# Attention over normalized tokens: merging the query and key projections, moving the value projection behind the softmax, and moving one routing step

## The chip, the cores and the metric

The kernel runs on one core of one Trainium2 chip. The metric is the device time of one execution in microseconds, the median over runs. A core has four compute engines, each with its own instruction queue that is worked off in order: TensorE (PE in the profile; PEld are its weight loads), VectorE (DVE), ScalarE (ACT) and GpSimd (POOL). SyncE (SP) here only issues DMAs. Queues wait for each other through semaphores. Matmuls write to PSUM; everything else lives in SBUF.

## What is computed

The input x is 2 x 64 x 64 tokens of 128 channels in float32. Four layers follow one another, each adding to x: a local attention with relative positions (layer 0), a triangular multiplication (layer 1), a gated causal attention and a feed-forward part in which 64 experts choose tokens (layer 2), and the layer of this study, layer 3. Its two halves, with t the tokens as 2 x 4096 x 128:

```python
def _L3_attn_ref(x, Wq, bq, Wk, bk, Wv, bv):
    TEMP = (2 * 128) ** 0.5
    q = jnp.einsum('bnf,of->bno', x, Wq) + bq
    k = jnp.einsum('bnf,of->bno', x, Wk) + bk
    v = jnp.einsum('bnf,of->bno', x, Wv) + bv
    scores = jnp.einsum('bnf,bmf->bnm', q, k) / TEMP
    alpha = jax.nn.softmax(scores, axis=-1)
    return jnp.einsum('bnm,bmf->bnf', alpha, v)

def _L3_ffn_ref(x, router_w, router_b, expert_w, expert_b):
    router_probs = jax.nn.softmax(x @ router_w + router_b, axis=-1)
    top_p, top_i = jax.lax.top_k(router_probs, K)          # K = 2 of E = 8
    top_p = top_p / jnp.sum(top_p, axis=-1, keepdims=True)
    expert_out = jnp.einsum('bnd,edc->bnec', x, expert_w) + expert_b
    gathered = jnp.take_along_axis(expert_out, top_i[..., None], axis=2)
    return jnp.einsum('bnk,bnkc->bnc', top_p, gathered)

t = t + _L3_attn_ref(_ln_t(t), ...)     # _ln_t: (v - mean) / sqrt(var + 1e-5)
t = t + _L3_ffn_ref(_ln_t(t), ...)
```

The attention has one head of width 128, is not causal, and has no output projection.

## The kernel before

**x stays in SBUF** for the whole kernel as `self.x`, 64 chunks of 128 tokens (128 partitions) by 128 channels. Constants: P = C = 128, L = 4096 tokens a batch, B = 2 batches, NC = 32 chunks and NB = 8 blocks of 512 tokens a batch, E2 = 8 experts. All matmuls are float32; the trace shows each of them as two passes, so that a matmul counts as x2.

**Layer 3's weights** are made early. `layers` (L1700 to L1734) opens a small pool at the start of layer 1, loads Wq, Wk, Wv and the biases on SP's queue ahead of layer 1's own weights, transposes the three matrices on TensorE after layer 1 was recorded (L1728 to L1731), and calls `l3_bound` (L1769 to L1810). This computes from the weights a bound on any score, so that the softmax may leave out the maximum. A register gets the answer; `layer3` (L1736 on) branches on it at L1763 between `l3_bounded`, which runs here, and `l3_any`, a general path that takes a softmax by rows.

**Layer 2's attention** (`layer2_attn`) is written with generators: its key groups, positions, block ends and so on are jobs, added by `add(key, pieces, generator)` in the loop at L1480 and following, and a planner lets a piece run between score steps according to how much is left (the pieces are costs, the loop's end is the due time). The order of the instructions on each engine is fixed by that when the program is built.

**Layer 3's attention** (`l3_bounded`, L1942 to L2076) walks over 2 batches x 8 blocks of 512 queries. Within a block there are 16 steps `k2`, each with two chunks of keys:
- scores: two matmuls at L2048 from kT (128 channels x 128 keys) and qT (512 queries) into the PSUM tile `sc`;
- exponentials on ACT at L2059 into `es` (three buffers, the first step's being the accumulator `acc`);
- of the step before (`values`, L2001 on): two matmuls at L2008 that add v^T es to the PSUM tile `oT`, and a DVE addition at L2016 that sums `es` into `acc` for the denominators.

Then `piece()` lets one step of the first waiting job run (two in the first block). The jobs:
- `keys` (`l3_qkv`, L1834): for a group of 512 tokens, statistics on DVE with a square root on ACT (`l3_stats`), normalization on DVE and four transposes on TensorE (`l3_transposed`, L1831) with a copy by ACT, then two projections (L1846, tiles `pk` and `pq`) with a bias pass by ACT each, and four matmuls for the values (L1853, tile `pv`) with an addition of bv by DVE at L1856. Batch 0's eight groups run in the first block, batch 1's one by one in the blocks of batch 0.
- `end` (L1974): DVE copies `oT`, GpSimd adds the two halves of `acc` (L1979, tile `both`), TensorE transposes the outputs back to tokens (L1983, tile `po`) and sums the denominators over partitions (L1986, `pr`), and DVE scales and adds to x (L1997).
- `logits` (`f3_logits`, L1860): statistics, normalization and transposes of the finished block, kept in `self.xnT`, and the router matmul (L1876).
- `route` (`f3_route`): the choice of two experts of 8 by maxima on DVE and an exponential on ACT; for 32 chunks of batch 0, for 28 of batch 1.
- `bias` (`f3_bias`, L1926): the chosen weights are copied by GpSimd into a padded tile, transposed (L1933), copied by ACT (L1935) and multiplied with the experts' biases (L1938); DVE adds the result to x (L1940).

After the last block the waiting jobs are run to their end, and then (L2071 to L2076) come `f3_route` for the last four chunks and the `f3_bias` of the last block.

**The experts** (`l3_experts`, L2127 on) take the 64 chunks one after the other. For each, two matmuls at L2142 make all eight experts' outputs in one two-bank PSUM tile `ex` (four buffers); DVE adds experts 0 to 3 with their weights to x (L2151, four instructions); ACT scales experts 4 to 7 into `y` (L2156, four); GpSimd sums these and adds them to x (L2162 to L2164); every fourth chunk 256 KB are written out.

Of the kernel before, what the change touches and what calls it, by code (L numbers as in the profile page):

```python
# [15 lines left out]
B = 2  # L16
# [23 lines left out]
class Net:  # L40
# [1022 lines left out]
    def layer2(self, kept, done):  # L1063
        nc, tc, ins = self.nc, self.tc, self.ins
        with tc.tile_pool(reuse_waits="tile", name="g2", bufs=1) as gp:
# [13 lines left out]
            self.layer2_attn(gate, kept)  # L1079
# [3 lines left out]
    def layer2_attn(self, gate, kept):  # L1083
# [4 lines left out]
        with ExitStack() as st:  # L1088
# [400 lines left out]
            for i, (b, qb) in enumerate(order):  # L1489
                finish(("prepare", i))  # L1490
                nk = 4 * qb + 4
                if i == 0:
                    for g in range(1, NB):
                        add(("keys", 0, g), 3, keys(0, g, add_back=(g == 7)))
                    add(("sums", 0), 0, add_up(0))
                if i == 4:
                    add(("stats", 1), 0, norm_stats(1))
# [202 lines left out]
    def layers(self):  # L1700
# [9 lines left out]
        with tc.tile_pool(reuse_waits="tile", name="l3w", bufs=1, side="right") as wp:  # L1710
            w = {}
            kp = kept.enter_context(
                tc.tile_pool(reuse_waits="tile", name="l12", bufs=1, side="right")
            )
            with (
                tc.tile_pool(reuse_waits="tile", name="l3s", bufs=1) as ap,
                tc.tile_pool(reuse_waits="tile", name="l3sp", bufs=1, space=PSUM) as ps,
            ):
                raw = {n: self.load(ap, f"r{n}", [P, C], ins[f"L3_attn_W{n}"]) for n in "qkv"}
                for n in "qk":  # L1720
                    w[f"b{n}"] = self.load(wp, f"b{n}", [P, 1], column(ins[f"L3_attn_b{n}"]))
                w["bv"] = self.load(wp, "bv", [P, C], row_bcast(ins["L3_attn_bv"], C))
                w["rw"] = self.load(wp, "rw", [P, E2], ins["L3_ffn_router_w"])
                w["rb"] = self.load(wp, "rb", [P, E2], row_bcast(ins["L3_ffn_router_b"], E2))
                space = self.layer1(xT, gst, na, nb, xp, kp)
                for n in "qkv":
                    pt = ps.tile([P, C], F32, tag="misc", name=f"l3w{n}")
                    nc.tensor.transpose(pt, raw[n], self.ident)  # L1728
                    w[n] = wp.tile([P, C], F32, tag=f"w{n}", name=f"l3w{n}T")
                    nc.scalar.copy(w[n], pt)  # L1730
                small = self.l3_bound(ap, ps, raw, w)  # L1731
            first.close()
            self.layer2(space, kept.close)
            self.layer3(w, small)  # L1734

    def layer3(self, weights, small):  # L1736
        nc, tc, ins = self.nc, self.tc, self.ins
        G = B * NC
        with ExitStack() as st:
# [23 lines left out]
            with tc.If(small > 0) as fits:  # L1763
                self.l3_bounded(weights)
# [4 lines left out]
    def l3_bound(self, ap, ps, raw, weights):  # L1769
# [6 lines left out]
        nc = self.nc  # L1776
        ab = ap.tile([P, 2, C], F32, tag="ab", name="l3ab")
        for i, (lhsT, rhs) in enumerate(((raw["k"], raw["q"]), (None, None))):
            m = ps.tile([P, C], F32, tag="misc", name=f"l3m{i}")
            if i:  # L1780
                lhsT = rhs = ab[:, 0, :]
            nc.tensor.matmul(m, lhsT=lhsT, rhs=rhs, start=True, stop=True)
            nc.vector.tensor_copy(ab[:, i, :], m)
        pv = ps.tile([P, 4], F32, tag="misc", name="l3mv")
        bq, bk = weights["bq"], weights["bk"]
        nc.tensor.matmul(pv[:, 0:1], lhsT=raw["q"], rhs=bk, start=True, stop=True)
        nc.tensor.matmul(pv[:, 1:2], lhsT=raw["k"], rhs=bq, start=True, stop=True)
        bb = ap.tile([P, 4], F32, tag="bb", name="l3bb")
        nc.vector.tensor_copy(bb[:, 0:2], pv[:, 0:2])
        nc.vector.tensor_tensor(bb[:, 0:2], bb[:, 0:2], bb[:, 0:2], ALU.mult)  # L1790
        nc.vector.tensor_tensor(bb[:, 2:3], bq, bk, ALU.mult)
        nc.vector.tensor_tensor(ab[:, 0, :], ab[:, 1, :], ab[:, 1, :], ALU.mult)
        nc.vector.tensor_reduce(bb[:, 3:4], ab[:, 0, :], AX.X, ALU.add)
        ones = ap.tile([P, 1], F32, tag="one", name="l3one")
        nc.vector.memset(ones, 1.0)
        pt = ps.tile([P, 4], F32, tag="misc", name="l3mt")
        nc.tensor.matmul(pt[:1], lhsT=ones, rhs=bb, start=True, stop=True)
        t = self.small.tile([1, 4], F32, tag="l3t", name="l3t", bufs=1)
        nc.vector.tensor_copy(t, pt[:1])
        total = self.small.tile([1, 1], F32, tag="bs1", name="l3s1")  # L1800
        root = self.small.tile([1, 1], F32, tag="bs2", name="l3s2")
        nc.vector.tensor_tensor(total, t[:, 2:3], t[:, 2:3], ALU.mult)
        nc.vector.tensor_tensor(t[:, 0:1], t[:, 0:1], t[:, 1:2], ALU.add)
        nc.vector.tensor_scalar(t[:, 0:1], t[:, 0:1], float(C), None, ALU.mult)
        nc.vector.tensor_tensor(total, total, t[:, 0:1], ALU.add)
        nc.vector.tensor_scalar(total, total, 15.0, None, ALU.mult)
        nc.scalar.activation(root, t[:, 3:4], AF.Sqrt)
        nc.vector.tensor_scalar(root, root, 1.25 * C * C, None, ALU.mult)
        nc.vector.tensor_tensor(total, total, root, ALU.add)
        return self.at_most("l3", total, 60.0**2 * 2.0 * C)  # L1810
# [13 lines left out]
    def l3_transposed(self, ap, ps, out, n0, mv, r, tag):  # L1824
# [3 lines left out]
        xn = ap.tile([P, 4, C], F32, tag="xn", name=f"{tag}xn", bufs=2)  # L1828
# [5 lines left out]
    def l3_qkv(self, ap, ps, w, b, g, qT, kT, v, tag):  # L1834
# [3 lines left out]
        n0 = b * NC + 4 * g  # L1838
        mv, r = self.l3_stats(ap, n0, t)
        yield  # L1840
        xT = ap.tile([P, 512], F32, tag="xT", name=f"{t}xT", bufs=2)
        self.l3_transposed(ap, ps, xT, n0, mv, r, t)
        yield
        for dst, n in ((kT, "k"), (qT, "q")):
            pq = ps.tile([P, 512], F32, tag="misc", name=f"{t}p{n}")
            nc.tensor.matmul(pq, lhsT=w[n], rhs=xT, start=True, stop=True)  # L1846
            nc.scalar.activation(
                dst[:, g * 512 : (g + 1) * 512], pq, AF.Identity, bias=w[f"b{n}"]
            )
            yield  # L1850
        pv = ps.tile([P, 4, C], F32, tag="misc", name=f"{t}pv")
        for i in range(4):
            nc.tensor.matmul(  # L1853
                pv[:, i, :], lhsT=xT[:, i * P : (i + 1) * P], rhs=w["v"], start=True, stop=True
            )
        nc.vector.tensor_tensor(  # L1856
            v[:, 4 * g : 4 * g + 4, :],
            pv,
            w["bv"].unsqueeze(1).broadcast_to([P, 4, C]),
            ALU.add,  # L1860
        )
# [81 lines left out]
    def l3_bounded(self, w):  # L1943
# [7 lines left out]
        with (  # L1951
# [22 lines left out]
            def end(b, qb, oT, acc):  # L1974
# [7 lines left out]
                for i in range(4):  # L1982
                    nc.tensor.transpose(po[:, i, :], os[:, i * P : (i + 1) * P], self.ident)  # L1983
# [20 lines left out]
            def values():  # L2004
# [12 lines left out]
                if k2 == NC // 2 - 1:  # L2017
# [6 lines left out]
                    jobs["logits", b, qb] = self.f3_logits(ap, ps, w, b, qb, "f3f")  # L2024
# [46 lines left out]
            for job in (  # L2071
                self.f3_route(ap, 2 * NC - 4, 4, "f3r2"),
                self.f3_bias(ap, ps, w, 2 * NB - 1, "f3f"),
# [137 lines left out]
```

## Time and profile before

| what | value |
|---|---|
| median of 3 runs | 4906.94 us (4905.28 to 4908.01) |
| the profiled execution | 4914.85 us |
| its span in the trace | 4913.0 us |
| mean granted TensorE clock | 0.954 |
| layer 0 | 0 to about 2173 us |
| layer 1 | to about 2368 us |
| layer 2, attention / feed-forward | to about 3620 / 3780 us |
| layer 3, attention | to about 4767 us |
| layer 3, rest of routing and biases | to about 4789.8 us |
| layer 3, experts and output | to the end |

The profile is of one execution. Its page gives, by engine, the busy time, then groups of instructions: line, engine, operation, output and inputs, shape and count, then after the first bar the busy time and the mean duration in ns, and after the second the idle time of the engine just before these instructions with what ended it. Where the idle time is 0.0 the engine went from one instruction to the next. The rows by stage give a window in us, its length, the busy time of PE, PEld, DVE, ACT and POOL with their counts, the granted clock as a share of full speed, the DMA share and GB/s. The chain of waits gives a start, a length and what ran or was waited for; "issue" is time for which the profile shows no wait.

### The profile page before, as it was taken

To read this page: it belongs to the slowest core of one execution; us is meant where nothing else is said; L and a number is where in the kernel's file an instruction comes from. 1 tells how busy PE (TensorE), PEld (TensorE's weight loads), DVE (VectorE), ACT (ScalarE), POOL (GpSimd) and SP (SyncE) were. 2 spreads that over 40 slices of the span, in tenths; PEclk is the share of its full clock that TensorE was granted. 3 is DMA by queue.
4 is the path that set the end of the run, shared out by engine and by line. 5 is a ranking of instruction groups with operands and counts; after the bars stand their busy time and mean duration, and the time that the engine had idled before them with its cause. 6 is when DMAs were issued, how large, how long until landed. Compare 5 with 4: busy or idle time off the path is not lost.

```text
span 4913.0 us, 78463 instructions
## 1 busy us (share of the span) xinstructions
PE 4556.6 (93%) x33360; PEld 1785.9 (36%) x33360; DVE 2937.1 (60%) x4864; ACT 2666.8 (54%) x3100; POOL 922.1 (19%) x832
## 2 busy tenths in 40 slices
PE   6999999999999999977789999999967999999999
PEld 4333333333233333325322223222225444444443
DVE  4676767676766767774755666555553444454447
ACT  4555555555656555555567766676631443333335
POOL 1000000000000000003355555555520000000008
PEclk7999999999999999988899999999978999999999
DMA  1000000000000000000000000000034000000001
GB/s 46 10 1 10 1 10 1 10 1 10 1 1 10 1 12 1 1 8 16 8 1 1 1 1 1 1 1 1 1 106 176 0 1 1 0 1 0 0 1 35
DMA packets 43355, 60.30 MB, mean 12 GB/s; under 512 B 4496, under 2 KB 25200, under 8 KB 41840
## 3 DMA queue, kind: packets, MB, share of 16 engines
q1 hardware_dynamic: 41696, 54.34, 3.5%
q8 instruction: 265, 4.34, 0.4%
q10 hardware_dynamic: 1296, 0.82, 0.1%
q14 instruction: 98, 0.80, 0.1%
HBM read 42.57 MB, written 4.19 MB: 10 GB/s over the span
## 4 chain that ended last, share of the span: by engine, by line
PE 38%; DVE 6%; ACT 3%; POOL 3%; issue 2%; DMA 0%; POOLq 0%; DVEq 0%; ACTq 0%
PE scl L2048 9%; PE oTl L2008 9%; PE l2sc L1422 5%; PE l2pos L1180 4%; PE l2av L1468 3%; PE f3ex L2142 2%; DVE l2es L1442 2%; POOL l2es L1445 2%; ACT l2es L1453 1%; ACT l2es L1433 1%; PE l2po L1388 1%; DVE l2a L169 0%; PE f3fpb L1938 0%; PE l2pu L1180 0%; PE f2pp L1613 0%
## 5 line engine op out<-in xcount | busy, mean ns | idle before, releaser
L597 DVE TENSOR_TENSOR l0es<-l0es,l0ew 128x1024 f32<-128x1024 f32 x1024 | 1251.9, 1227 | 603.3 <-ACT l0es L596 603.3
L596 ACT ACTIVATE l0es<-l0sc 128x1024 f32<-128x1024 f32 x1024 | 1043.5, 1024 | 721.9 <-PE l0sc L588 712.3
L546 PE MATMUL l0o<-l0es,l0v 64*33 64x512 f32 x8192 | 1069.8, 592 | 51.7 <-DVE l0os L556 46.4
L588 PE MATMUL l0sc<-l0qa,ka 64*64 64x512 f32 x8192 | 1081.9, 597 | 4.7 <-ACT l0es L596 4.6
L1453 ACT ACTIVATE l2es<-l2es 128x1024 f32<-128x1024 f32 (+3 forms) x576 | 560.0, 984 | 274.7 <-POOL l2es L1445 266.8
L1445 POOL TENSOR_TENSOR l2es<-l2es 128x1024 f32<-128x1024 f32 (+3 forms) x352 | 581.4, 1662 | 489.4 <-DVE l2es L1442 417.3
L2016 DVE TENSOR_TENSOR accl<-accl,esl 128x1024 f32<-128x1024 f32 x240 | 293.8, 1224 | 430.4 <-ACT esl L2059 426.5
L1442 DVE TENSOR_SCALAR l2es<-l2sc 128x1024 f32<-128x1024 f32 (+3 forms) x320 | 338.6, 1058 | 316.4 <-PE l2sc L1422 313.6
L2059 ACT ACTIVATE esl<-scl 128x1024 f32<-128x1024 f32 x240 | 245.8, 1024 | 472.5 <-PE scl L2048 446.7
L546 PEld LDWEIGHTS l0o<-l0es,l0v 64*33 64x33 f32 x8192 | 257.9, 108 | 659.4 <-issue 564.3
L588 PEld LDWEIGHTS l0sc<-l0qa,ka 64*64 64x64 f32 x8192 | 294.8, 133 | 547.4 <-issue 480.9
L2048 PE MATMUL scl<-l3qT,l3kT 128*128 128x512 f32 x1024 | 486.3, 595 | 0.0
L1422 PE MATMUL l2sc<-l2q,kept 32*128 32x512 f32 (+3 forms) x2304 | 391.7, 628 | 83.3 <-ACT l2es L1433 63.3
L2008 PE MATMUL oTl<-esl,l3v 128*128 128x512 f32 x960 | 450.9, 592 | 0.0
L722 POOL TENSOR_TENSOR x<-x,l0y 128x256 f32<-128x256 f32 x32 | 23.4, 732 | 2074.4 <-DVE l0y L717 1945.9
L1468 PE MATMUL l2av<-l2es,kept 128*32 128x512 f32 (+3 forms) x2304 | 314.8, 594 | 0.0
L1180 PE MATMUL l2pos<-kept 128*32 128x512 f32 x2416 | 297.3, 600 | 0.0
L2008 PEld LDWEIGHTS oTl<-esl,l3v 128*128 128x128 f32 x960 | 181.8, 190 | 225.8 <-issue 222.9
L2048 PEld LDWEIGHTS scl<-l3qT,l3kT 128*128 128x128 f32 x1024 | 186.9, 190 | 199.8 <-issue 186.0
L1433 ACT ACTIVATE l2es<-l2sc 128x1024 f32<-128x1024 f32 x224 | 226.4, 1010 | 48.6 <-PE l2sc L1422 47.1
L1422 PEld LDWEIGHTS l2sc<-l2q,kept 32*128 32x128 f32 x2304 | 117.1, 189 | 327.3 <-ACT l2es L1433 165.3
L1979 POOL TENSOR_TENSOR bothl<-accl 128x512 f32<-128x512 f32 x16 | 20.2, 1265 | 799.2 <-DVE accl L2016 799.2
(733 smaller groups left out, 3882.0 us busy)
## 6 DMA issues: line engine op xcount, KB each, us to landing
f2w<-in_L_ffn_weight_dram SPq DMA_DIRECT2D x32, 1024.0 KB, 13.5
l0ew<-l0ew SPq DMA_DIRECT2D x16, 512.0 KB, 5.1
x<-in_x_dram SPq DMA_DIRECT2D x8, 512.0 KB, 8.9
out_dram<-x SPq DMA_DIRECT2D x16, 256.0 KB, 2.3
kept<-in_L_attn_pos_rev_dram SPq DMA_DIRECT2D x1, 1792.0 KB
ew<-in_L_ffn_expert_w_dram SPq DMA_DIRECT2D x1, 512.0 KB, 4.0
kept<-in_L_attn_pos_rev_dram SPq DMA_DIRECT2D x1, 256.0 KB, 3.1
f2b<-in_L_ffn_weight_dram ACTq DMA_DIRECT2D x2, 128.0 KB, 2.5
```

What stands on the lines that cost most here:

```text
L546: nc.tensor.matmul(o[64 * h : 64 * h + HD + 1, r, :], lhsT=v1[rows, k, 2 * pair + h, :], rhs=es[rows, h, :], start=(k == 0), stop=(k == NC ...
L588: nc.tensor.matmul(sc[64 * c : 64 * c + 64, h, :], lhsT=ka[rows, k0 : k0 + 64], rhs=qa[rows, k // (NC // 2), qs], start=True, stop=True,)
L596: nc.scalar.activation(es, sc, AF.Exp)
L597: nc.vector.tensor_tensor(es, es, ew[:, :, qs], ALU.mult)
L1180: nc.tensor.matmul(out[part], lhsT=lhsT[:, part], rhs=rhs, start=start, stop=stop)
L1422: nc.tensor.matmul(sc[:, h2, off:], lhsT=kT[hs, k * P : (k + 1) * P], rhs=q[hs, off:], start=True, stop=True,)
L1442: nc.vector.tensor_scalar(es[:, :, lo:], sc[:, :, lo:], root, None, ALU.mult)
L1445: nc.gpsimd.tensor_tensor(part, part, part, ALU.mult)
L1453: nc.scalar.activation(es[:, :, off:], es[:, :, off:], AF.Silu)
L1468: nc.tensor.matmul(avs[i][hs, off:], lhsT=v[:, k, hs], rhs=es[h // 2][:, h % 2, off:], start=(k == 0), stop=last,)
L2008: nc.tensor.matmul(oT, lhsT=vs[b][:, k, :], rhs=es[:, i, :], start=(k == 0), stop=(k == NC - 1),)
L2048: nc.tensor.matmul(sc[:, i, :], lhsT=kTs[b][:, k * P : (k + 1) * P], rhs=qT[:, qb * 512 : (qb + 1) * 512], start=True, stop=True,)
```

## The change

With xn the normalized tokens, the scores are (Wq xn_i + bq) . (Wk xn_j + bk). Terms without j fall out of the softmax over j, which leaves (Wk^T Wq xn_i + Wk^T bq) . xn_j. So the keys can be xn itself, and one projection of the queries by the product of the two matrices holds all. In the same way Wv can be applied to the weighted sum of xn instead of to each xn, and bv, which is weighted by shares that sum to one, is added to x once.

The change does this in five places.
- `layers` no longer loads Wq, Wk, Wv, bq and bk at the start of layer 1 and no longer transposes or bounds there; `l3_bound` is gone. A new job `l3_weights` of four pieces in layer 2's attention, added at its third block (i == 2), loads them into space of layer 2's kept tile and makes Wv^T, Wq^T Wk and Wk^T bq, and a new bound from the latter two, without a square root. The register is loaded in its last pieces.
- `l3_qkv`: the normalized tokens are written straight into `v`, their transposes are copied into `kT`, one projection makes `qT`. GpSimd adds bv to x, 128 x 512.
- `end`: the four transposes of `po` become four matmuls with Wv^T on the right.
- The last block's `logits`, `route` and `bias` leave `l3_bounded`. A new generator `f3_late` holds them, and `l3_experts` runs one step of it ahead of every odd chunk.
- In `l3_experts` the PSUM tile `ex` has three buffers instead of four; two banks serve the late job.

`l3_any` is adapted as well; it doesn't run here.

```diff
+    def l3_weights(self, ap, ps, w, take):
+        nc, ins = self.nc, self.ins
+        raw = {n: take([C]) for n in "qkv"}
+        for n in "qkv":
+            nc.sync.dma_start(out=raw[n], in_=ins[f"L3_attn_W{n}"])
+        bq = self.load(ap, "rbq", [P, 1], column(ins["L3_attn_bq"]))
+        yield
+        pt = ps.tile([P, 512], F32, tag="misc", name="l3wps")
+        nc.tensor.transpose(pt[:, :C], raw["v"], self.ident)
+        nc.tensor.matmul(pt[:, C : 2 * C], lhsT=raw["q"], rhs=raw["k"], start=True, stop=True)
+        nc.tensor.matmul(pt[:, 2 * C : 2 * C + 1], lhsT=raw["k"], rhs=bq, start=True, stop=True)
+        nc.vector.tensor_copy(w["v"], pt[:, :C])
+        nc.vector.tensor_copy(w["qk"], pt[:, C : 2 * C])
+        nc.vector.tensor_copy(w["bqk"], pt[:, 2 * C : 2 * C + 1])
+        yield
+        pt = ps.tile([P, 512], F32, tag="misc", name="l3nps")
+        nc.tensor.matmul(pt[:, :C], lhsT=w["qk"], rhs=w["qk"], start=True, stop=True)
...
+        ok = self.small.tile([1, 1], mybir.dt.int32, tag="bok", name="bok_l3")
+        nc.vector.tensor_scalar(ok, t[:, 0:1], 0.0, None, ALU.is_gt)
+        yield
+        yield
+        w["small"] = nc.values_load(
...
     def l3_qkv(self, ap, ps, w, b, g, qT, kT, v, tag):
...
+        cols = slice(g * 512, (g + 1) * 512)
         mv, r = self.l3_stats(ap, n0, t)
         yield
-        xT = ap.tile([P, 512], F32, tag="xT", name=f"{t}xT", bufs=2)
-        self.l3_transposed(ap, ps, xT, n0, mv, r, t)
+        self.l3_transposed(ap, ps, kT[:, cols], n0, mv, r, t, v[:, 4 * g : 4 * g + 4, :])
         yield
-        for dst, n in ((kT, "k"), (qT, "q")):
-            pq = ps.tile([P, 512], F32, tag="misc", name=f"{t}p{n}")
-            nc.tensor.matmul(pq, lhsT=w[n], rhs=xT, start=True, stop=True)
...
-        pv = ps.tile([P, 4, C], F32, tag="misc", name=f"{t}pv")
...
+        pq = ps.tile([P, 512], F32, tag="misc", name=f"{t}pq")
+        nc.tensor.matmul(pq, lhsT=w["qk"], rhs=kT[:, cols], start=True, stop=True)
+        nc.scalar.activation(qT[:, cols], pq, AF.Identity, bias=w["bqk"])
+        xs = self.x[:, n0 : n0 + 4, :]
+        nc.gpsimd.tensor_tensor(xs, xs, w["bv"].unsqueeze(1).broadcast_to([P, 4, C]), ALU.add)
         yield
...
                 for i in range(4):
-                    nc.tensor.transpose(po[:, i, :], os[:, i * P : (i + 1) * P], self.ident)
+                    nc.tensor.matmul(
+                        po[:, i, :],
+                        lhsT=os[:, i * P : (i + 1) * P],
+                        rhs=w["v"],
+                        start=True,
+                        stop=True,
+                    )
...
-                    jobs["logits", b, qb] = self.f3_logits(ap, ps, w, b, qb, "f3f")
+                    if (b, qb) != (B - 1, NB - 1):
+                        jobs["logits", b, qb] = self.f3_logits(ap, ps, w, b, qb, "f3f")
...
             while jobs:
                 piece()
-            for job in (
-                self.f3_route(ap, 2 * NC - 4, 4, "f3r2"),
-                self.f3_bias(ap, ps, w, 2 * NB - 1, "f3f"),
-            ):
-                for _ in job:
-                    pass
...
+    def f3_late(self, ap, ps, w):
+
+        g4 = B * NC // 4 - 1
+        yield from self.f3_logits(ap, ps, w, B - 1, NC // 4 - 1, "f3l")
+        yield from self.f3_route(ap, 4 * g4, 4, "f3l")
+        yield from self.f3_bias(ap, ps, w, g4, "f3l")
...
-            tc.tile_pool(reuse_waits="tile", name="f3p", bufs=4, space=PSUM) as ps,
+            tc.tile_pool(reuse_waits="tile", name="f3p", bufs=2, space=PSUM) as ps,
+            tc.tile_pool(reuse_waits="tile", name="f3b", bufs=1) as bp,
         ):
+            late = self.f3_late(bp, ps, w)
             for n in range(B * NC):
+                if n % 2:
+                    next(late, None)
                 b, k = divmod(n, NC)
-                ex = ps.tile([P, E2, C], F32, tag="ex", name=f"f3ex{n}")
+                ex = ps.tile([P, E2, C], F32, tag="ex", name=f"f3ex{n}", bufs=3)
```

## The prediction

> **What bounds the kernel now.** I read the page's engine totals and costliest groups first, then busy time by stage, then the chain of waits in one stretch of layer 3's attention and at its end.
>
> ```profile
> PE 4556.6 (93%) x33360; PEld 1785.9 (36%) x33360; DVE 2937.1 (60%) x4864; ACT 2666.8 (54%) x3100; POOL 922.1 (19%) x832
> ...
> L2016 DVE TENSOR_TENSOR accl<-accl,esl 128x1024 f32<-128x1024 f32 x240 | 293.8, 1224 | 430.4 <-ACT esl L2059 426.5
> ...
> L2048 PE MATMUL scl<-l3qT,l3kT 128*128 128x512 f32 x1024 | 486.3, 595 | 0.0
> L1422 PE MATMUL l2sc<-l2q,kept 32*128 32x512 f32 (+3 forms) x2304 | 391.7, 628 | 83.3 <-ACT l2es L1433 63.3
> L2008 PE MATMUL oTl<-esl,l3v 128*128 128x512 f32 x960 | 450.9, 592 | 0.0
> ...
> L1979 POOL TENSOR_TENSOR bothl<-accl 128x512 f32<-128x512 f32 x16 | 20.2, 1265 | 799.2 <-DVE accl L2016 799.2
> ```
>
> Both big matmul groups of layer 3 (L2048, L2008) have no idle time before them; layer 2's scores (L1422) do wait. The stages, with PE, PEld, DVE, ACT and POOL busy and then the granted clock:
>
> ```profile
> 2640.00:2960.00 320.00, 295.94 (x2271) 92.81 (x2260) 191.85 (x399) 223.44 (x237) 174.05 (x113) 0.96 0.00 1
> ...
> 3872.00:4357.00 485.00, 485.00 (x1344) 230.88 (x1344) 227.89 (x576) 195.36 (x209) 11.76 (x10) 1.00 0.00 1
> 4357.00:4762.00 405.00, 405.00 (x1074) 189.09 (x1074) 178.09 (x379) 138.56 (x147) 11.45 (x14) 1.00 0.00 0
> 4762.00:4790.00 28.00, 18.65 (x59) 8.29 (x58) 13.89 (x53) 6.63 (x14) 2.53 (x7) 0.90 0.01 2
> 4790.00:4913.00 123.00, 112.34 (x256) 49.22 (x256) 89.81 (x256) 73.22 (x256) 102.23 (x192) 0.96 0.12 35
> ```
>
> Layer 3's attention is TensorE alone, every microsecond of it, at full clock, with DVE under half busy and ACT at 40%. A microsecond of PE taken out there is one off the kernel. The chain while the first block makes its keys (start, us, what):
>
> ```profile
> 3822.77 1.72 PE oTl L2008 x4
> 3824.49 0.44 PE l3f_4t L1831 x4
> 3824.93 1.72 PE scl L2048 x4
> 3826.65 1.72 PE oTl L2008 x4
> 3828.36 0.86 PE l3f_4pk L1846 x2
> 3829.22 0.86 PE l3f_4pq L1846 x2
> 3830.08 1.08 PE l3f_4pv L1853 x8
> 3831.16 1.72 PE scl L2048 x4
> ```
>
> A group of 512 keys costs 0.44 + 0.86 + 0.86 + 1.08 = 3.24 us beside its four 1.72 us pieces. The end of the attention:
>
> ```profile
> 4779.85 0.45 PE f3f_7t L1831 x4
> ...
> 4788.06 0.70 DVE x L1940
> 4788.76 1.00 issue
> 4789.76 10.45 PE f3ex L2142 x18
> ```
>
> From the last block's transposes to the first expert matmul, one serial chain (logits, choice, bias) runs with nothing beside it.
>
> **The change part by part.** The profiled execution took 4914.85 us, its span 4913.0. The median of the runs is 4906.94, so I make the sum on the profiled one and take it off the median.
>
> Attention, keys. Each of 16 groups loses one projection (0.86) and the value projection (1.08): 16 x 1.94 = -31.0. One ACT pass (0.69) and one DVE add (0.69) go too, beside PE work, for nothing. At the block ends, four transposes (0.44) become matmuls by Wv in the form of the value projection (1.08): 16 x 0.64 = +10.3. **Sum -20.8.** It checks on a block: a block of batch 0 is 16 x 3.434 (scores and values) + 3.24 (keys) + 0.79 + 0.44 (end) + 1.23 (logits) = 60.6, and L1979 starts every 60.65. After, 59.3; in batch 1 57.4 becomes 58.0; the first block sheds 15.5. In that block a score now waits on transposes, ACT's copy (0.59), one projection and one ACT pass (0.69); the transposes stand a score pair ahead of their use, so the copies hide behind 1.72 us pieces. Were they exposed in each of the 8 groups, it would be 8 x 0.6 = +5 at most.
>
> GpSimd's adds. The value bias goes into x on GpSimd, 128x512, 16 times; the nearest row is L1979 at 1.265. GpSimd is nearly idle there (11.8 of 485), and x is needed only at its block's end. Here a rule speaks against the change: the Trainium skill, "SBUF — State Buffer", section "Who interferes with whom", says that a DVE instruction with two SBUF inputs and a GpSimd instruction that reads SBUF exclude each other, one waiting for the whole of the other. The accumulation L2016 has two SBUF inputs. L1979 never runs beside it (it waits for it), so no row shows this. By L1979's row the 16 adds cost nothing; by the rule, if each delay reached PE, 16 x 1.265 = +20, the whole gain. I take 0: DVE is 47% busy, an accumulation has 3.4 us and takes 1.22, and three buffers stand between it and ACT. Bounds 0 to +20, by the slack near 0.
>
> Tail. Before, the last bias of the waiting seven ends in a DVE add at 4780.58, then come logits, choice and bias until 4788.75, then 1.00 us to the first expert matmul. After, the seven biases follow the block end directly: +0.64 for Wv (counted above), then the same 1.6 us apiece, so the add ends at 4780.6 on the old clock and experts start near 4781.7. **-8.1.**
>
> Experts. The last block's statistics, logits, choice and bias now run there: PE +2.2 (0.44 + 0.79 + 0.12 + 0.86), DVE +6.4 by their rows in the tail, POOL +0.2, and ACT a square-root and an exp table load (1.28 each). Their PSUM buffers fall from 4 to 3. In steady state a tile takes PE 1.72, DVE 4 x 0.351 plus issue = 1.51, POOL 0.73 + 0.46 + 0.46 with issue = 1.75, without gaps from the second tile: GpSimd is the bound, PE 0.03 behind. A buffer lives 3.2 us past its matmuls (DVE 0.2 + 1.51, ACT 0.1 + 1.14, release 0.25) against 2 x 1.72 = 3.43 with three: 0.23 slack, where four had 1.95. So what DVE does late goes through to GpSimd. At the start, DVE does the statistics (3.75 with the wait for ACT) before its first tile, and I get GpSimd's first add 6.7 us after the first matmul, where it was 6.6. In tiles 4 to 7 logits and choice put 2 to 2.5 us on DVE, in tiles 12 to 15 the bias 0.9 on PE and 0.7 on DVE. Against that stands the start: the first twelve expert matmuls took 0.85 apiece instead of 0.43 (4.9 us), of which GpSimd saw about 1.1 as a gap. The skill's "TensorE: Matmul & The Clock Gate", "What's actually happening", has the clock halve after an idle window of about 3.4 us. Before, PE stood still 3.0, 0.4 and 1.7 us between 4782 and 4790; after, once, about 1.7. By the rows (a gap halves it) the start stays slow and costs nothing new; by the rule it keeps its clock and GpSimd wins the 1.1. I take the 1.1: +3.3 - 1.1 = **+2**, between -2 and +8.
>
> Layer 1's start. Its seven loads, the transposes, the bound and their DVE and ACT steps leave. DVE sets the time there until 2208; about 1.1 us of l3ab and l3bb copies and of a wait for the square root stand in its queue: **-1.1** (0 to -2). The weight loads stand in another order on SP's queue (two of the five wide ones now behind bv, rw, rb, some 1.3 us later, just ahead of their use).
>
> Layer 2. The weights' product is made there: 0.9 us of PE, 2.6 of DVE, three loads on SP ahead of layer 2's own (issued around 2342, behind a 23.6 us pair; layer 2's first waits for other work until 2366.4, which hides them; uncovered, 3 x 0.45 = 1.4). PE's queue is in order, so a small matmul that waits for a DVE copy holds the scores behind it, 0 to 1.5 us twice. More than that, the job moves the planner's other pieces through the layer. PE is 92% busy there; its waits are 83 us. A shift is as likely to save as to cost; bounds -4 to +6, taken **+1**.
>
> Sum: -20.8 - 8.1 + 2 - 1.1 + 1 = **-27**. On the profiled execution 4888; from the median 4906.9 - 27 = **4880**.
>
> **The rivals.** The experts give the tail back: with 0.23 us of slack every late piece of DVE passes through, and +8 comes in place of +2: 4886. For it: the buffer's arithmetic. Against: late pieces lie apart, one step every second tile.
>
> The port: accumulations wait on GpSimd's adds and ACT and PE with them: -27 + 20 = 4900. Against: half of DVE is idle.
>
> Slower: layer 2's schedule falls out of step. Its L1422 waits of 83.3 us grow by half, +41.6, since pieces come between squared scores and their release (L1433): 4921. From +27 it eats the gain. Against: four small pieces among thousands of matmuls.
>
> It does not take the bounded path: the new test compares (1.25 C^2)^2 times the squared norm of the Gram matrix with the bias side squared. Worked from the inputs these are 1.7e11 and 8.5e11, so it passes. Failing would be far slower (a softmax by 128 queries with transposed probabilities); under 1 in 100.
>
> **How the numbers follow.** 0.2% of this kernel, 10 us, is about what a measurement can tell from no change. Forecast, 4872 to 4887: 63%. Layer 2 or a warm expert start gain more, down to 4867: 12%. The experts give back more or part of the keys' gain is exposed, 4887 to 4897: 17%. The port or a worse schedule, 4897 to 4917: 5%. Slower: 3%. Faster 0.92, same 0.05, slower 0.03. The range 4867 to 4893 leaves out some 15 in 100.
>
> **What would show it.** In the first block the key groups lie 8.16 us apart (10.10 before), blocks 59.3 and 58.0, L2048 and L2008 still with no idle time; the accumulation still at 1.22. The first expert matmul comes about 8 us sooner after the last block, GpSimd shows gaps near tiles 4 to 7, and the stage from there is 2 us longer. I am wrong if PE idles in the first block, if the accumulation stretches beside GpSimd, or if layer 2 moves by over 6 us.

## The result and the profile after

The changed kernel takes 4879.43 us, the median of 4 runs (4875.38 to 4883.02), against 4907.48 (4905.28 to 4911.56) for the kernel before, measured again beside it: a ratio of 0.994, 95% interval 0.9928 to 0.9952. That is 28.1 us less; the forecast was 4880, 27 less.

Its profiled execution took 4879.15 us with a span of 4877.3. The page's lines that answer to those of before:

```profile
PE 4514.3 (93%) x33260; PEld 1766.5 (36%) x33260; DVE 2943.3 (60%) x4845; ACT 2647.6 (54%) x3077; POOL 943.7 (19%) x848
...
L2014 DVE TENSOR_TENSOR accl<-accl,esl 128x1024 f32<-128x1024 f32 x240 | 302.6, 1261 | 425.8 <-ACT esl L2058 422.4
...
L2047 PE MATMUL scl<-l3qT,l3kT 128*128 128x512 f32 x1024 | 486.8, 595 | 0.0
L1422 PE MATMUL l2sc<-l2q,kept 32*128 32x512 f32 (+3 forms) x2304 | 389.4, 619 | 88.6 <-ACT l2es L1433 65.3
L2006 PE MATMUL oTl<-esl,l3v 128*128 128x512 f32 x960 | 450.9, 592 | 0.0
...
L1971 POOL TENSOR_TENSOR bothl<-accl 128x512 f32<-128x512 f32 x16 | 20.2, 1263 | 633.6 <-DVE accl L2014 633.6
```

TensorE has still no idle time in layer 3's attention (the 0.0 of L2047 and L2006), so it has only less to do. The accumulation's mean rose from 1224 to 1261 ns: something stands in its way that wasn't there before. Layer 2's scores wait 88.6 us instead of 83.3. The stages (window, length, then busy time of PE, PEld, DVE, ACT, POOL, then the granted clock):

```profile
2398.00:3606.00 1208.00, 1102.57 (x8171) 352.66 (x8167) 717.38 (x1327) 838.18 (x891) 660.50 (x462) 0.95 0.00 1
...
3783.00:4732.50 949.50, 949.50 (x2570) 448.15 (x2571) 444.98 (x1051) 361.17 (x389) 44.44 (x39) 1.00 0.00 0
4732.50:4752.70 20.20, 14.69 (x47) 6.35 (x46) 8.04 (x14) 4.09 (x9) 2.31 (x6) 1.00 0.01 3
4752.70:4877.30 124.60, 114.51 (x271) 50.46 (x271) 94.99 (x296) 75.17 (x262) 102.35 (x193) 0.96 0.12 35
```

To compare stages between kernels I use marks that all have: the ends of layer 0's and layer 2's scores, the first and last score of layer 3, and the first expert matmul. One execution each:

| stage | before | after | difference |
|---|---|---|---|
| layer 0's last value matmul to layer 1's main projection | 74.8 | 69.2 | -5.6 |
| from there to layer 2's first score | 163.0 | 161.9 | -1.1 |
| layer 2, first to last score | 1207.3 | 1207.5 | +0.2 |
| to layer 3's first score | 179.6 | 177.6 | -2.0 |
| layer 3, first to last score | 970.5 | 949.6 | -20.9 |
| to the first expert matmul | 27.6 | 20.2 | -7.4 |
| experts, to the end of the span | 123.2 | 124.6 | +1.4 |

Layer 0's end differs by 0.3. The lines from layer 2's scores on sum to -28.7, close to the timed difference of -28.1. Layer 1's -5.6 and the -1.1 behind it come on top in these two executions; the profiled one of before was 7.4 us above its median, that of the changed kernel at its median. An experiment below goes into that.

In the first block the chain of waits of the changed kernel reads:

```profile
3801.58 0.44 PE l3f_3t L1836 x4
3802.01 1.72 PE scl L2047 x4
3803.73 1.72 PE oTl L2006 x4
3805.45 0.86 PE l3f_3pq L1850 x2
3806.31 1.72 PE scl L2047 x4
3808.02 1.72 PE oTl L2006 x4
3809.74 0.44 PE l3f_4t L1836 x4
```

A key group comes every 8.16 us, as forecast, and TensorE goes from one piece to the next without a gap. The end of the attention:

```profile
4749.20 1.14 PE f3fpb L1930 x2
4750.34 0.02 issue
4750.36 0.70 DVE x L1932
4751.06 1.66 issue
4752.72 7.08 PE f3ex L2156 x12
4759.81 0.44 PE f3l_7t L1836 x4
```

The experts follow the seventh bias, with no choice in between, but 1.66 us after its addition (`issue`: the profile shows nothing that is waited for). The last block's transposes now stand between expert matmuls.

### The profile page after: what moved, and what is told of

Read it like the earlier page. It is cut to its first block, busy times and chain, and to the rows that moved or that the text cites. A ratio compares the mean times of both kernels' runs of the same rounds, so it can differ in the third digit from the quotient of the medians.

```text
span 4877.3 us, 78242 instructions
## 1 busy us (share of the span) xinstructions
PE 4514.3 (93%) x33260; PEld 1766.5 (36%) x33260; DVE 2943.3 (60%) x4845; ACT 2647.6 (54%) x3077; POOL 943.7 (19%) x848
## 4 chain that ended last, share of the span: by engine, by line
PE 37%; DVE 6%; ACT 3%; POOL 3%; issue 2%; DMA 0%; POOLq 0%; DVEq 0%; ACTq 0%
PE scl L2047 9%; PE oTl L2006 9%; PE l2sc L1422 5%; PE l2pos L1180 4%; PE l2av L1468 3%; PE f3ex L2156 2%; DVE l2es L1442 2%; POOL l2es L1445 2%; ACT l2es L1453 1%; ACT l2es L1433 1%; PE l2po L1388 1%; DVE l2a L169 0%; PE f3fpb L1930 0%; PE pol L1975 0%; PE l2pu L1180 0%
## 5 line engine op out<-in xcount | busy, mean ns | idle before, releaser
L2014 DVE TENSOR_TENSOR accl<-accl,esl 128x1024 f32<-128x1024 f32 x240 | 302.6, 1261 | 425.8 <-ACT esl L2058 422.4
L2047 PE MATMUL scl<-l3qT,l3kT 128*128 128x512 f32 x1024 | 486.8, 595 | 0.0
L1422 PE MATMUL l2sc<-l2q,kept 32*128 32x512 f32 (+3 forms) x2304 | 389.4, 619 | 88.6 <-ACT l2es L1433 65.3
L2006 PE MATMUL oTl<-esl,l3v 128*128 128x512 f32 x960 | 450.9, 592 | 0.0
L2047 PEld LDWEIGHTS scl<-l3qT,l3kT 128*128 128x128 f32 x1024 | 188.5, 191 | 208.2 <-issue 192.5
L2006 PEld LDWEIGHTS oTl<-esl,l3v 128*128 128x128 f32 x960 | 181.8, 190 | 225.8 <-issue 221.5
L1971 POOL TENSOR_TENSOR bothl<-accl 128x512 f32<-128x512 f32 x16 | 20.2, 1263 | 633.6 <-DVE accl L2014 633.6
```

The source lines that it names most:

```text
L1422: nc.tensor.matmul(sc[:, h2, off:], lhsT=kT[hs, k * P : (k + 1) * P], rhs=q[hs, off:], start=True, stop=True,)
L2006: nc.tensor.matmul(oT, lhsT=vs[b][:, k, :], rhs=es[:, i, :], start=(k == 0), stop=(k == NC - 1),)
L2047: nc.tensor.matmul(sc[:, i, :], lhsT=kTs[b][:, k * P : (k + 1) * P], rhs=qT[:, qb * 512 : (qb + 1) * 512], start=True, stop=True,)
```

## The experiments

**Attention alone.** The last block's logits, choice and bias go back behind the attention, with four expert buffers. The weights are still made in layer 2.

```diff
-            late = self.f3_late(bp, ps, w)
...
-                ex = ps.tile([P, E2, C], F32, tag="ex", name=f"f3ex{n}", bufs=3)
+                ex = ps.tile([P, E2, C], F32, tag="ex", name=f"f3ex{n}")
```

> The changed kernel with the last block's logits, choice and bias put back behind the attention and four expert buffers, so only the merged projections and Wv at the block ends are left. If TensorE's time in the attention is the gain: from the first score to the last 949.6 us as in the changed kernel (970.5 before), then 23.6 us to the first expert matmul and 123.2 from there, as before; in all about 4907 - 22 = 4885, that is 6 us above the changed kernel. If the gain came from layer 2's shifted schedule or from layer 1, the attention would still be near 970.

Measured: 4882.63 against 4906.18 for before, ratio 0.996 (0.9946 to 0.9973), so -23.6. First to last score 949.4, from there to the experts 28.3, experts 122.2. The attention's part stands by itself and layer 2 (1208.4) has none of it. The experts' stage has the code of before and is about 1 us shorter: here the clock was full 3.0 us after its first matmul, before 5.0 us after it.

**The late choice alone**, in the kernel before:

```diff
+            late = self.f3_late(bp, ps, w)
             for n in range(B * NC):
+                if n % 2:
+                    next(late, None)
```

> The kernel before with only the late choice: last block's logits, choice and bias between the experts, three expert buffers. If the tail is a serial chain that the experts absorb: 16.2 us from the last value matmul's end to the first expert matmul (23.6 before), then 124.6 to the end (123.2), in all about 4901. If the experts give it all back (the rival): 131 from there and 4907. Layer 1 and 2 are those of before, so the layer 1 clock is a further look at it with the weights' preparation in place.

Measured: 4901.52, ratio 0.999 (0.9982 to 0.9999), -4.7. Attention 970.4, to the experts 20.0 (27.6 before), experts 125.9 (123.2). The tail gives 7.6 and the experts take 2.7 back, 1.3 more than expected; at their start the half clock lasted 6.8 us, in the changed kernel 3.4. The rival, all given back, is out, though the interval (-8.8 to -0.5) reaches close to nothing. The two halves, -23.6 and -4.7, add up to -28.3; the whole change gave -28.1. Each has an interval of several us, so that only a large effect of one on the other is ruled out.

**The merged projection without moving Wv**: values projected as before, transposes at the block ends.

```diff
+            nc.tensor.matmul(
+                pv[:, i, :],
+                lhsT=kT[:, g * 512 + i * P : g * 512 + (i + 1) * P],
+                rhs=w["v"],
...
-                    nc.tensor.matmul(
-                        po[:, i, :],
...
+                    nc.tensor.transpose(po[:, i, :], os[:, i * P : (i + 1) * P], self.ident)
```

> The changed kernel with the values projected as before (v = xn Wv + bv, added by DVE) and transposes at the block ends; left are the merged query-key projection and the late choice. If each matmul taken out counts with its own duration, the attention loses 16 x 0.86 = 13.8 us to before: from first to last score about 957, in all about 7 us above the changed kernel, 4886. With no addition on GpSimd the accumulation should be back at 1.225 us at most. If moving Wv to the block ends is worth nothing (its matmuls at the ends cost as much as they save): 4879.

Measured: 4886.35, ratio 0.9963 (0.9949 to 0.9976); first to last score 956.7 (957 expected). So the merge is worth 13.8 and Wv at the block ends 7.1 of the 20.9. And without GpSimd's addition of bv the longest accumulation is 1.228 us; in the changed kernel it is 2.226.

**GpSimd's addition three times.** The changed kernel's trace shows what stretches: GpSimd's addition beside an accumulation and beside normalizations. First GpSimd, then DVE, in the changed kernel:

```profile
3802.17 1.30 POOL L1853 TENSOR_TENSOR x<-x,bv 128x512 f32<-128x512 f32 x1 [4.40 <-DVE l3v L169]
3804.14 2.18 POOL L1853 TENSOR_TENSOR x<-x,bv 128x512 f32<-128x512 f32 x1 [0.68 <-DVE l3v L169]
...
3862.35 1.27 POOL L1853 TENSOR_TENSOR x<-x,bv 128x512 f32<-128x512 f32 x1 [14.57 <-DVE l3v L169]
```

```profile
3802.00 2.06 DVE L169 TENSOR_SCALAR l3v<-x,l3f_7mv,l3f_7r 128x128 f32<-128x128 f32 x4
...
3862.48 3.54 DVE L2014 TENSOR_TENSOR accl<-accl,esl 128x1024 f32<-128x1024 f32 x2 [0.22 <-ACT esl L2058]
```

At 3862 GpSimd is first, and two accumulations take 3.54 us instead of 2.4; at 3804 DVE is first, and GpSimd's addition takes 2.18 instead of 1.27. Four normalizations at 3802 take 2.06 instead of 1.12. One stands still while the other runs. So I tripled the addition:

```diff
-        nc.gpsimd.tensor_tensor(xs, xs, w["bv"].unsqueeze(1).broadcast_to([P, 4, C]), ALU.add)
+        for op in (ALU.add, ALU.subtract, ALU.add):
+            nc.gpsimd.tensor_tensor(xs, xs, w["bv"].unsqueeze(1).broadcast_to([P, 4, C]), op)
```

> The changed kernel with GpSimd's addition of the value bias to x done three times (plus, minus, plus), 32 additions of 1.27 us more. The trace of the changed kernel shows accumulations beside GpSimd stretched from 1.23 to 2.23. If the slack of DVE hides that: total DVE accumulation time rises by some 20 us, and the attention from first to last score stays within 2 us of 949.6. If the port reaches TensorE (the rival): up to 32 x 1.27 = 40 us more, most of it in the first block, where eight groups follow each other.

Measured: 4888.69, ratio 0.9969 (0.9957 to 0.998), about 9 us above the changed kernel; first to last score 957.4 (+7.8), the accumulations 311.3 us in all instead of 302.6. Neither expectation holds: it reaches TensorE, but with a fifth of the 40 us. The windows show where, first with three additions, then in the changed kernel:

```profile
3780.00:3800.00 20.00, 18.74 (x44) 8.38 (x43) 20.00 (x72) 10.66 (x15) 14.51 (x11) 0.85 0.00 0
3800.00:3820.00 20.00, 15.65 (x39) 6.92 (x38) 19.02 (x40) 8.96 (x12) 17.40 (x11) 0.91 0.01 1
3820.00:3840.00 20.00, 20.00 (x54) 9.19 (x53) 6.13 (x5) 7.73 (x11) 2.53 (x2) 1.00 0.00 0
...
3860.00:3920.00 60.00, 60.00 (x165) 28.36 (x164) 29.18 (x63) 24.25 (x26) 6.79 (x4) 1.00 0.00 0
```

```profile
3780.00:3800.00 20.00, 19.96 (x47) 9.14 (x48) 19.89 (x93) 12.98 (x19) 7.55 (x6) 0.89 0.00 0
3800.00:3820.00 20.00, 20.00 (x57) 9.45 (x56) 10.97 (x24) 9.47 (x12) 3.48 (x2) 1.00 0.00 1
```

With three additions DVE (third figure) is full for 40 us, 20.00 and 19.02 of 20; with one it is full for the first 20 only. Most of what PE lacks in the first window lies ahead of the first score (3782.3). In the second it has one long wait, here with what ACT did before it:

```profile
3804.48 1.28 ACT L95 ACT_TABLE_LOAD   x1 [6.87 <-DVE rs_v L93]
...
3809.03 2.91 PE L2007 MATMUL oTl<-esl,l3v 128*128 128x512 f32 x4 [4.35 <-ACT esl L2059]
```

ACT has a square root of the statistics in its queue and stands 6.87 us until DVE delivers its input (L93). The exponentials follow it, and PE waits 4.35 us for them. The remainder of the 7.8 us is mostly clock: full clock comes 3.8 us after the first score instead of 1.3, and half clock follows the wait for 3.41 us; by estimate from these times that is another 2.9. From 3820 on DVE has half its time free, GpSimd's three additions run through, and PE is at 60.00 of 60. The lock costs where DVE falls so far behind that others wait for it: at the start of the phase, when it makes statistics for eight groups. With one addition a group, PE does not wait there.

**Four expert buffers with the late choice**: its PSUM tiles take turns in one ring with the expert tiles.

```diff
-            late = self.f3_late(bp, ps, w)
+            late = self.f3_late(bp, Ring(ps), w)
```

> The changed kernel with four expert buffers again: the late job's PSUM tiles take turns in the same ring of four. If three buffers let DVE's late pieces through to GpSimd (the forecast's reason for +2): from the first expert matmul to the end 123.5 instead of 124.6. If three are enough and the rest is the start and GpSimd's own extra copy: 124.5, nothing to see in the total (within 1 us of the changed kernel, 4880).

Measured: 4880.15, ratio 0.9941 (0.9924 to 0.9957), experts 124.2 against 124.6, where the forecast's reason asked for 123.5. The third buffer less is a small part of the experts' cost.

**Late choice later**, from chunk 9 on.

```diff
-                if n % 2:
+                if n > 8 and n % 2:
                     next(late, None)
```

> The changed kernel with the late job's first step ahead of chunk 9 instead of chunk 1. In the changed kernel DVE does the statistics and the normalization (3.7 us) ahead of its first tile, and GpSimd, the bound, gets its first tile 7.0 us after the first expert matmul. If that is what sets the start: GpSimd starts at about 5.0 to 5.5 and the stage takes 123 us instead of 124.6. If the half clock of the first ten expert matmuls sets it: GpSimd starts near 6.4, its second tile waits, and the stage takes 124 or more.

Measured: 4879.68, ratio 0.9946 (0.9929 to 0.9963), experts 124.7, GpSimd's first tile after 7.0. But the edit didn't do what it says. Its trace on DVE:

```profile
4748.12 0.49 DVE L1823 BATCH_NORM_STATS2 f3l_7st<-x 128x6 f32<-128x128 f32 x2
...
4750.83 0.86 DVE L169 TENSOR_SCALAR f3l_7xn<-x,f3l_7mv,f3l_7r 128x128 f32<-128x128 f32 x3
4751.61 0.34 DVE L2165 SCALAR_TENSOR_TENSOR x<-f3ex,f3wt,x 128x128 f32<-128x128 f32 x1
```

Statistics and most of the normalization are still ahead of the first tile (L2165): the instructions' order isn't that of the Python lines. The run says nothing on what sets the start.

**Two job pieces per step in the last block**, so that the seven biases run inside the attention.

```diff
-                        if b == 0 and qb == 0:
+                        if (b, qb) in ((0, 0), (B - 1, NB - 1)):
                             piece()
```

> The changed kernel with two job pieces per step in the last block too, so that the seven biases run inside the attention. There a bias costs TensorE 0.96 us, behind the attention 1.64 (a chain of PE, ACT, PE). If that is so: attention from first to last score +6.7, to 956, the tail from the last score to the first expert matmul from 20.2 to 9.5, in all -4 against the changed kernel, 4875. If DVE or ACT are too full for twelve routing pieces at double pace, TensorE waits in the last block and nothing is won.

Measured: 4878.69, ratio 0.9943 (0.9926 to 0.9959). The attention is 953.6 (+4.0), the tail 13.6 (-6.6): in the trace -2.6 (-4 was expected), in the time -0.7, within its spread. Four of the seven biases moved into the attention; routing took the other places. Each costs TensorE 0.97 us there instead of 1.64.

**No branch.** The bounded path is taken always; the general path is left out.

```diff
-            with tc.If(weights["small"] > 0) as fits:
-                self.l3_bounded(weights)
-            with fits.Else():
-                self.l3_any(weights)
+            self.l3_bounded(weights)
```

> The changed kernel without the branch: the bounded path is taken always, the general path (a softmax by rows) is left out. It tests what the 1.0 to 2.4 us of 'issue' ahead of the first expert matmul are. If they are the end of the branch: PE goes from the last bias to the experts in about 0.7 us (its DVE addition), the tail is 1.7 us shorter (18.5), the last 1 to 2 us at the start of the phase may go as well; in all -2 to -4. If they are a wait for PSUM or SBUF that the trace doesn't name, the tail stays 20.2.

Measured: 4874.81, ratio 0.9935 (0.9918 to 0.9951). The way to the first score is 172.5 instead of 177.6 and the attention 3.0 longer, since some key work now lies behind the first score; the tail is 18.7 (-1.5), GpSimd's first tile comes after 4.9 instead of 7.0, the experts take 123.3. PE stands still for 0.78 us ahead of the experts instead of 2.40. So the 1.66 us of "issue" belong to the end of the branch. What it does in that time isn't shown.

**Experts inside the branch.** That barrier can go without giving up the general path: each side of the branch calls the experts itself. With the two pieces of above:

```diff
             with tc.If(weights["small"] > 0) as fits:
                 self.l3_bounded(weights)
+                self.l3_experts(weights)
             with fits.Else():
                 self.l3_any(weights)
-            self.l3_experts(weights)
+                self.l3_experts(weights)
```

> The changed kernel with the experts called inside each side of the branch instead of behind it, and two job pieces per step in the last block. Without the branch the tail was 1.5 us shorter, GpSimd's first tile 2.1 us sooner and the experts 1.3 shorter. If the end of the branch is what held them: tail under 12 (13.6 with two pieces alone), GpSimd's first tile near 5, experts 123; in all 3 to 5 us under the changed kernel, 4875. If it was the branch's start alone: 4878.

Measured: 4873.00 (4870.44 to 4877.69), ratio 0.9929 (0.9915 to 0.9942), 34 us under before where the change is 28. Tail 11.9, GpSimd's first tile after 4.9, experts 123.2. Its chain at the same place:

```profile
4747.44 0.70 DVE x L1933
4748.14 0.04 issue
4748.18 3.71 PE f3ex L2157 x8
```

The 1.66 us are 0.04. DVE makes the last block's first statistics at 4744.4, ahead of the last bias; in the changed kernel nothing of the late choice starts before 4753.2, behind the branch. So DVE's first tile comes 2.0 us after the first expert matmul instead of 4.1, and GpSimd's sooner with it.

**The weights' preparation alone.** Every trace with layer 3's preparation at layer 1's start showed a longer layer 1 (74.8 and 75.8) than those without it (69.0 to 71.2). So: the kernel before, with only this part moved into layer 2.

```diff
-                for n in "qkv":
-                    pt = ps.tile([P, C], F32, tag="misc", name=f"l3w{n}")
-                    nc.tensor.transpose(pt, raw[n], self.ident)
...
+                    add(("layer 3",), 4, self.l3_weights(wp, ps, w3, take))
```

> The kernel before with one thing of the change: layer 3's weights are made in layer 2's attention instead of at layer 1's start (three transposes instead of one, the new bound). Attention, tail and experts stay as before. All traces with the preparation in layer 1 show 74.8 to 75.8 us from layer 0's last matmul to layer 1's main projection, those without it 69.0 to 71.2, with a half TensorE clock for 5 to 7 of its steps against 1 to 5. If that holds in the timed runs as well: 4901, that is 5 us under the kernel before. If it is a matter of the profiled executions (which were 8 us above the median in both kernels with the preparation there, and at the median in the others): 4905 to 4906, 0 to 1 under it, while the trace shows 69 to 71.

Measured: 4908.93 (13 runs), ratio 1.0003 (0.9995 to 1.0011); its trace has 71.3 in layer 1. In the runs' time the move shows no gain; the interval goes from 2.5 us less to 5.4 more.

**The kernel before again**, for a second profile.

> The kernel before once more, for a second profile of it. If layer 1's slow clock with the preparation is its own: 74 to 76 us from layer 0's last matmul to the main projection again. If it is chance: anything from 69 to 76.

Measured: 4906.80, ratio 0.9997 (0.9989 to 1.0006); layer 1 took 75.1 in its trace, which was 4.7 us above its median. In the first trace of before and in that of the changed kernel the same steps of layer 1, transposes and projection of one group:

```profile
2225.00 1.06 PE L443 MATMUL l1pt<-ident,xT 128*128 128x128 f32 x4
2226.92 2.08 PE L897 MATMUL l1pg<-xT,wcat 128*128 128x512 f32 x2 [0.87 <-ACT xT L444]
```

```profile
2225.57 0.60 PE L443 MATMUL l1pt<-ident,xT 128*128 128x128 f32 x4
2227.18 1.13 PE L897 MATMUL l1pg<-xT,wcat 128*128 128x512 f32 x2 [1.01 <-ACT xT L444]
```

The work is the same, at half clock above and at full below. All three profiles with the preparation there have the clock come up at the seventh or eighth group; of the ten without it, nine have it come up at the second to the sixth, and that of the moved preparation goes up, down and up again. Yet the runs of the moved preparation show no gain in time. One execution of each kernel has a trace, so how long layer 1 takes in the others isn't known. Whether the preparation there keeps the clock slow, or these traces had it so by chance, stays open.

## Why the prediction was right, step by step

**Attention, -20.8.** Right in its mechanism and 2 us short in size: -20.9 between the scores and -1.9 ahead of them (from layer 2's last matmul to the first score 10.8 instead of 12.7), together -22.8. I took the 1.08 us of the value projection in the first block for both the removed and the new matmuls. Of these 1.08, 0.19 are a wait. The first weight load of `pv` stands until ACT has emptied `pk` into kT, with two PSUM buffers for three tiles that follow each other (before, then the merged projection alone):

```profile
3819.89 0.97 PEld L1853 LDWEIGHTS l3f_3pv<-l3wvT,l3f_3xT 128*128 128x128 f32 x8 [0.75 <-ACT l3kT L1847]
```

```profile
3808.06 0.86 PE l3f_3pq L1850 x2
3808.92 0.89 PE l3f_3pv L1855 x8
```

PE's idle time of 0.0 doesn't show this wait, as the profile lets the matmuls' durations overlap. With one projection less, the same eight matmuls in the same place take 0.89, as they do in batch 1's groups before the change and at the block ends after it. So the keys give 8 x (0.86 + 1.08) + 8 x (0.86 + 0.89) = 29.5 instead of 31.0, and the 15 block ends ahead of the last score cost 15 x (0.89 - 0.44) = 6.75, where I had 10.3 for 16: -22.8, as measured. That this is so close is partly chance, since the first group's matmuls run at half clock in both. The block of batch 0 is 59.35 (59.3 forecast).

**GpSimd's additions, 0 of a possible +20.** Right in its value and in its reason, the slack: PE has no idle time there. But one of the forecast's own signs of being wrong came true. The accumulation was to stay at 1.22, and it stretched. The rule that spoke against the change holds: the Trainium skill, "SBUF — State Buffer", "Who interferes with whom", says one of the two waits for the whole of the other, and the trace shows it (1.23 to 2.23, and GpSimd's 1.27 to 2.18 where DVE was first). The slack hid the wait, and the tripled addition found its limit: with DVE full for 40 us, 8 us were lost.

**Tail, -8.1 and 0.64.** Measured -7.4, close to their sum of -7.5. The serial chain is gone; the pause ahead of the experts grew from 1.00 to 1.66, where the forecast had 1.1.

**Experts, +2.** Measured +1.4, and +2.7 with the late choice alone. The size was near, and the late pieces do come through to GpSimd: it starts 0.4 later, and it stands 0.65, 0.17, 0.15 and 0.32 us ahead of tiles 4, 6, 7 and 15 (counted from 0), where the forecast put these pieces. Before, it stood once, 0.60 ahead of tile 1. The buffers have a small share in this. With three and full clock (the tripled addition) these stops sum to 0.95, with four and full clock to 0.63.

The term that was wrong is the 1.1 us for a warm clock. (Its working misread the start before: six matmul passes were slow there, not twelve.) In the changed kernel the weight loads of the first expert matmuls stand 0.43 apart, the next ones 0.85 until 4757. The Trainium skill, "TensorE: Matmul & The Clock Gate", "What's actually happening", puts the half clock behind an idle window of about 3.4 us; here PE had stood still for 2.40. But the length of the stop alone doesn't decide. Seven traces have one of 2.40 to 2.65 us here. In five of them half clock follows; in two, the tripled addition (2.63) and the four buffers (2.45), the clock stays full. Five us from the first expert matmul, in the changed kernel and in these two:

```profile
4752.70:4757.70 5.00, 4.98 (x8) 2.21 (x9) 3.94 (x22) 0.27 (x2) 0.00 (x0) 0.66 0.02 5
```

```profile
4760.20:4765.20 5.00, 4.99 (x12) 2.32 (x13) 3.97 (x22) 0.21 (x1) 0.00 (x0) 1.00 0.02 5
```

```profile
4755.70:4760.70 5.00, 4.97 (x12) 2.33 (x13) 3.91 (x21) 0.20 (x1) 0.00 (x0) 1.00 0.02 5
```

What decides stays open. These two also show what a warm clock would have brought: GpSimd's first tile still comes 7.0 and 7.1 us after the first matmul, behind DVE's statistics, and the stage takes 124.6 and 124.2. Where DVE has no such work ahead of its first tile, the clock does seem to count: with the attention alone it was full 2 us sooner than before, and the stage was 1 us shorter. With the experts inside the branch the stop is 0.78, and the first eight take 3.71, full clock.

**Layer 1, -1.1; layer 2, +1.** In the runs' time neither is seen (the preparation alone, with two transposes more than in the change: ratio 0.9995 to 1.0011, that is -2.5 to +5.4 us). The trace of layer 1 shows -5.6 by the clock, for which I had no step. Layer 2 between its scores is +0.2, although its waits rose by 5.3 us. As the kernel before itself has 1207.3 and 1201.8 there in two executions, nothing finer can be said. The rival of a schedule out of step (+41.6) is out.

**The sum, -27.** That it comes within about 1 us of the measured -28.1 is partly luck. The attention gave 2 more than forecast, the tail 0.7 less, the experts cost 0.6 less, and the terms of layers 1 and 2, which cancel, are too small to be seen.

## What to carry to other kernels

Where one engine is busy every microsecond of a stage at full clock, the durations of the instructions taken out are the gain. But look for waits hidden in them: the same eight matmuls cost 0.89, or 1.08 us where their weight load waits for a buffer. Work that moves onto another engine is free only while the engine that shares its port can catch up before the busy engine waits for it. That is to be asked of the fullest stretch, not of the stage's mean: here one stretch of 20 us with DVE full cost nothing, one of 40 us cost 8. The end of a branch holds the stage behind it, so what follows it is better called inside both sides: 1.7 us at this one, and GpSimd's first tile 2.1 us sooner.

## What was not expected of the hardware

Executions of one program differ by layer: layer 0, the same code in all kernels here, ended between 2161.1 and 2167.4 us, and layer 2's scores took 1201.8 to 1208.9. A difference of a few microseconds in one stage of two traces is no finding unless that stage repeats it over several, as layer 3's attention does within 1 us (970.4, 970.4, 970.5, 970.5 in the kernels with the old one; 949.4, 949.6, 949.6, 950.2 in those with the new, where nothing else in it was changed).

Half clock comes in steps. In the 13 traces it is granted in 493 stretches, and all but twelve, each the last of its trace, take 3.41 us or a multiple of it (6.83, 10.24 and so on). It may be that the place of a stop in this beat decides whether half clock follows, as with the seven stops ahead of the experts; no run here varied that alone.
